# Four-head graph attention: transposed aggregation in 32-column groups, and an order of the engines found by list scheduling

## The chip, the cores and the metric

The kernel runs on one core of one Trainium2 chip. The metric is the device time of one execution in microseconds (us). The program is a straight line of instructions: five engines (TensorE as PE, VectorE as DVE, ScalarE as ACT, GpSimd as POOL, SyncE as SP) each work through a fixed queue and wait for each other by semaphores. On PE a matmul is two instructions, a weight load ("PEld" in the profile) and the matmul itself ("PE"); each fp32 matmul that is no transpose makes two such pairs of records.

## The reference, cut to what matters

Thirty-two batches of 512 nodes with 256 features pass through four graph-attention layers, each with a layer norm ahead of it and a residual sum after it. The change concerns the third layer, which has four heads of 64 features:

```python
    def _L2_gnn_ref(h, adj, W, a):
        N_H, D_F = (4, 64)
        Wh = (h @ W).reshape(h.shape[0], h.shape[1], N_H, D_F)
        ...
        e = s_src[:, :, None, :] + s_dst[:, None, :, :]
        e = jnp.where(e > 0, e, NEG_SLOPE * e)
        e = jnp.where(mask, e, -jnp.inf)
        alpha = jax.nn.softmax(e, axis=2)
        h_out = jnp.einsum('bijh,bjhd->bihd', alpha, Wh)
        ...
        return jax.nn.elu(h_out)
```

For each head, every node i takes an average of the other nodes' 64 features, weighted by a softmax over its neighbours j. The other layers have one head of 256 or 512 features, and the fourth also has two dense layers.

## The kernel before, in words

**Streams.** The batches are dealt out to four streams (`NS = 4`), each with one batch at a time, and started 75 us apart in the program's own time (`LEAD`). `batch`, `layer0` to `layer3` are generators: they emit instructions for a step and yield a time at which the stream wants to go on. The loop at the end of `fast` always advances the stream with the earliest time, so the four batches stand at different layers and their instructions are mixed. The order in which the program is written comes from this; the tile framework then sorts the instructions of each engine by its own simulation, except where `keep_in_program_order` ties one down. [...]

**Attention without a division by the softmax's sum first.** A batch is four tiles of 128 nodes (`NT = 4`). For every head, `weights` makes the matrix of unnormalised weights, `w`, with the source nodes j on the partitions: four DVE instructions of 128x512 (L353), one for each tile j, each the maximum of a row (spread over all partitions) and a column, times the mask. Of the four heads, the first row comes from PE transposes into a PSUM bank, the other three through DRAM (`rows_out`, `spread`) with SP's DMAs. The values `v` carry an exponential factor in column D, so that a matmul with D + 1 columns gives the sum of weights as well.

**Layer 2's aggregation.** For each head and each target tile t, `aggregate` adds up four matmuls over j: `w` (128x128) is the stationary operand, `v` with its 65 columns the moving one. Four tiles t share one PSUM bank. DVE then takes a reciprocal of the four sums (L387) and multiplies (L497) into `ya`, a tile with one buffer of its own. After every second head ACT makes the exponential and the ReLU (L504, L505), and `add_elu` (L405, L406) adds the ELU to `x`.

**Resources shared by all streams.** Eight PSUM banks, two for each stream, where a stream may also use those of an idle stream (`bank`). SBUF buffers of the tag "w" (four, for the weights of all layers), "y" (three), "q" (three), "g", "sums" and others. SP issues all plain DMAs: x, row and spread, sums from the sorted order (L614), the table (L647, L648), and the output (L716). POOL issues the indirect DMAs (L607, L655) and adds the residual of the last layer (L715).

Of the kernel before, what the change touches and what calls it, by code (L numbers as in the profile page):

```python
# [8 lines left out]

# [1 line left out]

# [6 lines left out]
FP = mybir.dt.float32  # L20
BF = mybir.dt.bfloat16
# [3 lines left out]
OP = mybir.AluOpType  # L25
AX = mybir.AxisListType
# [5 lines left out]
TINY = 1.0e-30  # L32
CYCLES = 2400.0

@with_exitstack
def fast(ctx, tc, flag, x, adj, w0, a0, w1, a1, w2, a2, mlp1_w, mlp1_b, mlp2_w, mlp2_b,
         w_fc, a_fc, w_hand, a_hand, out):
# [10 lines left out]
    SLOW = 1.5  # L48
    STRETCH = 2.0

    const = ctx.enter_context(tc.tile_pool(name="const", bufs=1))
    work = ctx.enter_context(tc.tile_pool(name="work", bufs=2))
    psum = ctx.enter_context(tc.tile_pool(name="psum", bufs=1, space=bass.MemoryType.PSUM))
    dram = ctx.enter_context(tc.tile_pool(name="dram", bufs=1, space=bass.MemoryType.DRAM))

    turn = [0]
    begun = [0.0]
# [7 lines left out]
        spent[0] += 4 * max(x.shape[-1], P)  # L65
        nc.tensor.matmul(p, w, x, **flags)  # L66

    def transpose(p, x, i, tied=False):
        spent[0] += 2 * P
        instruction = nc.tensor.transpose(p, x, i)  # L70
        if tied:
            tc.keep_in_program_order(instruction)

    active = set()
    banks = [0]
# [131 lines left out]
    def setup():  # L207

        own = work.tile([P, NT, N], FP, tag="w", name="own", bufs=4)
        nc.vector.tensor_scalar(own, adj_sb, 0.0, None, op0=OP.is_gt)  # L210
        nc.gpsimd.affine_select(
            out=own, in_=own, pattern=[[P, NT], [-1, N]], base=0, channel_multiplier=1,
            compare_op=OP.not_equal, fill=1.0,
        )
        tc.keep_in_program_order(nc.vector.tensor_reduce(differ[:, 0:1], adj_sb, AX.XY, OP.min))
        nc.vector.tensor_scalar(differ[:, 0:1], differ[:, 0:1], 0.0, None, op0=OP.is_lt)
        for j in range(NT):
            turn[0] = NS - 1 - j % (NS - 1)
            p = bank()
            for t in range(NT):  # L220
                transpose(p[:, t * P:(t + 1) * P], own[:, t, j * P:(j + 1) * P], ident, j + t == 0)
            nc.scalar.copy(maskT[:, j, :], p)
        turn[0] = NS - 1
        yield
        yield from finish_w(fetched1, 0.01)


        least = small([1], "rden")
        nc.vector.tensor_reduce(least, diag, AX.X, OP.min)
        nc.vector.tensor_scalar(differ[:, 1:2], least, 0.0, None, op0=OP.is_le)  # L230
        nc.vector.tensor_copy(W2[:, :, :, :D], raw2.rearrange("p k (h d) -> p k h d", d=D))
        nc.vector.tensor_scalar_mul(A2v[:, :, 1:2], A2v[:, :, 0:1], -0.8)
        nc.vector.tensor_scalar_mul(A2v[:, :, 2:3], A2v[:, :, 2:3], 0.8)
        for k in range(KF):
            project(W2[:, k, :, D:], lambda k, f: raw2[:, k, f * P:(f + 1) * P], k, A2)
            yield
        yield from finish_w(fetched3, 0.2)

        for tri, sign in ((before, 1), (after, -1)):
            nc.vector.memset(tri, 1.0)  # L240
            nc.gpsimd.affine_select(
                out=tri, in_=tri, pattern=[[sign, P]], base=0, channel_multiplier=-sign,
                compare_op=OP.is_gt, fill=0.0,
            )
        ties = work.tile([P, 2 * N - P], FP, tag="w", name="ties", bufs=4)
        nc.vector.memset(ties, TINY)
        nc.gpsimd.affine_select(
            out=ties, in_=ties, pattern=[[-1, 2 * N - P]], base=N - P, channel_multiplier=1,
            compare_op=OP.is_gt, fill=0.0,
        )  # L250
        nc.vector.tensor_copy(band, ties)
        yield
        yield from finish_w(fetched4, 0.2)
# [89 lines left out]
    def weights(r_col, t_col, masked=True, r=None):  # L343

        landed = r is not None
        if not landed:
            r = bank()
            for t in range(NT):
                transpose(r[:, t * P:(t + 1) * P], r_col(t).to_broadcast([P, P]), ident)
        wt = work.tile([P, NT, N], FP, tag="w", name="w", bufs=4)  # L350
        for j in range(NT):
            if masked:
                w = nc.vector.scalar_tensor_tensor(  # L353
                    wt[:, j, :], r, t_col(j), maskT[:, j, :], op0=OP.max, op1=OP.mult
                )
                if landed and j == 0:
                    tc.keep_in_program_order(w)
            else:
                nc.vector.tensor_scalar(wt[:, j, :], r, t_col(j), None, op0=OP.max)
        return wt  # L360
# [22 lines left out]
            matmul(p, wt[:, j, t * P:(t + 1) * P], rhs(j), start=(j == 0), stop=(j == NT - 1))  # L383

    def reciprocal(den):
        r = small([1], "rden") if len(den.shape) == 2 else small([NH, 1], "rden4")
        nc.vector.reciprocal(r, den)  # L387
        return r

# [62 lines left out]
    def layer2(xt, xn, rs, when):  # L452
        hT = yield from turned(xn, when)
        v = work.tile([P, NT, NH, CH], FP, tag="v", name="v2", bufs=4)
        for t in range(NT):
            ps = bank()
            for k in range(KF):
                matmul(
                    ps[:, :NH * CH], hT[:, k, t * P:(t + 1) * P], W2[:, k, :, :], start=(k == 0), stop=(k == KF - 1)
                )  # L460
            pv = ps[:, :NH * CH].rearrange("p (h c) -> p h c", c=CH)
            nc.scalar.activation(v[:, t, :, D:], pv[:, :, D:], AF.Exp, scale=rs[:, t:t + 1])
            nc.vector.scalar_tensor_tensor(  # L463
                v[:, t, :, :D], pv[:, :, :D], rs[:, t:t + 1], v[:, t, :, D:D + 1].to_broadcast([P, NH, D]),
                op0=OP.mult, op1=OP.mult,
            )
            yield after_us(0 if t + 1 < NT else 1)
        ya = work.tile([P, NT, F], FP, tag="y4", name="y4", bufs=1)
        wts = []

        def begin(h):
            wts.append(
                weights(
                    lambda t: v[:, t, h, D + 2:D + 3], lambda j: v[:, j, h, D + 1:D + 2], r=far[h]
                )
            )
            return after_us(3.2)

        row_d = rows_out(v[:, :, :, D + 2], NH)
        far = [spread(row_d[h, :]) if h else None for h in range(NH)]
        when = begin(0)
        note(v.rearrange("p t h c -> p (t h) c")[:, :, D:])
        yield after_us(3)
        for h in range(NH):
            last = when
            if h + 1 < NH:
                when = begin(h + 1)
            yield last  # L490
            wt = wts[h]
            p = bank()
            for t in range(NT):
                aggregate(p[:, t * (D + 1):(t + 1) * (D + 1)], wt, t, lambda j: v[:, j, h, :D + 1])
            pv = p[:, :NT * (D + 1)].rearrange("p (t c) -> p t c", c=D + 1)
            r = reciprocal(pv[:, :, D:])
            nc.vector.tensor_tensor(  # L497
                ya[:, :, h * D:(h + 1) * D], pv[:, :, :D], r.to_broadcast([P, NT, D]), op=OP.mult
            )
            if h % 2:  # L500
                c = slice((h - 1) * D, (h + 1) * D)
                y = ya[:, :, c]
                q = pair("q").rearrange("p a (b f) -> p (a b) f", f=2 * D)
                nc.scalar.activation(q, y, AF.Exp)  # L504
                nc.scalar.activation(y, y, AF.Relu)  # L505
                add_elu(xt[:, :, c], y, q)
            yield after_us(0)
        xn, rs = new_xn(), small([NT], "rs")
        for t0 in range(0, NT, 2):
            norm(xt, xn, rs, t0, False)  # L510
        yield after_us(7)
        return xn, rs, after_us(2)
# [50 lines left out]
    def sort_attend(oT, b):  # L563
# [31 lines left out]
            project_half(oT, halves, ends, 1, t)  # L595
            yield after_us(0)
        for t in range(NT):
            junk = work.tile([P, N], BF, tag="junk2", name="junk2", bufs=1)
            nc.scalar.activation(
                junk, tj, AF.Sign, bias=ends[:, t, 2:3], scale=-1.0, accum_out=found[:, 1, t:t + 1]  # L600
            )
# [17 lines left out]
        for c in range(2):  # L619
# [2 lines left out]
            u = sums[:, :, 1, :]  # L622

            T = small([NT], "T")
            tc.keep_in_program_order(nc.vector.tensor_copy(T, u[:, :, F + 1]))
            tot = work.tile([P, C], FP, tag="tot", name="tot", bufs=1)
            nc.vector.tensor_tensor(sums[:, 2, 0, :], u[:, 0, :], u[:, 1, :], op=OP.add)
            nc.vector.tensor_tensor(sums[:, 3, 0, :], sums[:, 2, 0, :], u[:, 2, :], op=OP.add)
            nc.vector.tensor_tensor(tot, sums[:, 3, 0, :], u[:, 3, :], op=OP.add)
# [34 lines left out]
        for t in range(NT):  # L664
# [1 line left out]
            y, q = pair(), pair("q")  # L666
            g = gs[t]
            z = g[:, :2 * C]
            tc.keep_in_program_order(
                nc.vector.scalar_tensor_tensor(z, z, ends[:, t, 2:3], g[:, 2 * C:], op0=OP.mult, op1=OP.add)  # L670
            )
            rd = reciprocal(z[:, F:F + 1])
            z = z.rearrange("p (c n) -> p c n", c=2)[:, :, :F]
            nc.scalar.activation(q, z, AF.Exp, scale=rd)
# [122 lines left out]
    one = const.tile([1, 1], FP, name="one")  # L797
    nc.vector.tensor_reduce(one, p[:1, :P], AX.X, OP.max)
    nc.vector.tensor_scalar(flag, one, 0.5, None, op0=OP.is_gt)


@with_exitstack
# [430 lines left out]
```

## Time and profile before

| What | us |
|---|---|
| median of 3 runs (2934.32 to 2936.52) | 2936.34 |
| span of the profiled execution, first to last instruction | 2929.6 |
| PE busy | 2858.9 |
| PE weight loads busy | 2329.5 |
| DVE busy | 2219.9 |
| ACT busy | 1536.8 |
| POOL busy | 502.3 |

The profile is of one execution; its own time is known as the span, and the profile gives nothing beyond it, so that what lies before the first and after the last instruction can only be taken as the distance to the median, 6.7 us. A line of the profile names the source line, the engine, the operation, the output and input tiles by name, the shape, the count and then busy time and the mean of one in ns, or what the sentence ahead of it says. `L66` is the helper `matmul`, `L70` the helper `transpose`; so PE's rows are told apart by their tiles and shapes. The row of 128x65 (4096 records, mean 273 ns) is layer 2's aggregation. The granted TensorE clock was 0.996 of full speed.

### The profile page before, as it was taken

The page shows a single profiled execution, that of the slowest core. Times are in us where ns is not written, and L with a number is a line of the kernel's source. Part 1 is how long each engine was busy: PE and PEld are TensorE (multiplying, and loading weights), DVE is VectorE, ACT ScalarE, POOL GpSimd, SP SyncE. Part 2 cuts the span into 40 slices and gives each one's busy share as a digit, 9 for nine tenths or more (in the row PEclk, how much of TensorE's full clock was granted, in tenths as well). Part 3 has the DMA queues.
Part 4 walks back from the last instruction along what each step waited for, and adds up shares of the span by engine and source line. Part 5 has one row for each costly group of instructions (what it writes and reads, how often), then busy time and mean ns, then how long its engine had stood idle before and what let it go on. Part 6 is the DMA issues. An engine that isn't in the chain of part 4 may idle for free.

```text
span 2929.6 us, 43083 instructions
## 1 busy us (share of the span) xinstructions
PE 2858.9 (98%) x15177; PEld 2329.5 (80%) x15177; DVE 2219.9 (76%) x5676; ACT 1536.8 (52%) x3922; POOL 502.3 (17%) x515
## 2 busy tenths in 40 slices
PE   8999999999999999999999999999999999999998
PEld 6777887877888877888877888788887788877876
DVE  4677877778778778778778777787787787777764
ACT  4444455555555555555554556545555555555444
POOL 0011112112122111122021121111221111211220
PEclk9999999999999999999999999999999999999999
DMA  3033223233223333233332233222332322323230
GB/s 94 19 102 102 80 88 116 91 98 95 88 94 106 93 100 98 84 102 96 100 102 80 89 115 93 91 97 91 94 116 80 102 93 88 104 93 96 90 107 30
DMA packets 193182, 270.89 MB, mean 92 GB/s; under 512 B 17024, under 2 KB 156094, under 8 KB 192960
## 3 DMA queue, kind: packets, MB, share of 16 engines
q1 hardware_dynamic: 163200, 169.76, 18.5%
q0 software_dynamic: 29760, 98.30, 10.4%
q8 instruction: 123, 2.02, 0.3%
q14 instruction: 99, 0.81, 0.1%
HBM read 152.62 MB, written 115.39 MB: 91 GB/s over the span
## 4 chain that ended last, share of the span: by engine, by line
PE 82%; DVE 10%; ACT 4%; DMA 3%; issue 1%; SPq 0%; POOL 0%; DVEq 0%; POOLq 0%; ACTq 0%
PE b L66 75%; PE b L70 7%; DVE st L269 2%; DMA g<-table,at 2%; DVE sums L641 1%; DVE xn L280 1%; DVE x L406 1%; DVE y L405 1%; ACT v L325 1%; DVE sums L632 1%; ACT y L505 1%; ACT q L504 1%; DVE w L353 1%; ACT hT L290 1%; DVE tot L646 0%
## 5 line engine op out<-in xcount | busy, mean ns | idle before, releaser
L66 PE MATMUL b<-v,w 128*128 128x65 f32 (+1 forms) x7232 | 1218.0, 321 | 10.6 <-DVE w L353 10.5
L66 PEld LDWEIGHTS b<-v,w 128*128 128x128 f32 x7232 | 1050.0, 191 | 168.7 <-issue 56.1
L66 PE MATMUL b<-WFC,oT 128*128 128x256 f32 (+1 forms) x2048 | 495.2, 380 | 0.0
L66 PEld LDWEIGHTS b<-WFC,oT 128*128 128x128 f32 x2048 | 374.5, 189 | 49.3
L66 PE MATMUL b<-W,hT 128*128 128x259 f32 (+1 forms) x1536 | 388.8, 391 | 22.8 <-DVE v L463 14.1
L353 DVE SCALAR_TENSOR_TENSOR w<-b,v,maskT 128x512 f32<-128x512 f32 x512 | 369.4, 744 | 5.1 <-PE b L70 4.1
L607 POOL DMA_INDIRECT order<-v,at x248 | 277.0, 1117 | 490.7 <-DVE oT L730 152.3
L66 PEld LDWEIGHTS b<-W,hT 128*128 128x128 f32 x1536 | 285.3, 192 | 75.3 <-DVE v L463 17.1
L715 POOL TENSOR_TENSOR x<-x,y 128x512 f32<-128x512 f32 x62 | 87.8, 1416 | 1063.7 <-ACT y L713 950.0
L353 DVE SCALAR_TENSOR_TENSOR w<-spread,v,maskT 128x512 f32<-128x512 f32 x384 | 269.5, 742 | 0.0
L66 PE MATMUL b<-hT,WM 128*128 128x512 f32 x512 | 250.0, 599 | 0.7 <-ACT hT L290 0.7
L66 PE MATMUL b<-oT,WM 128*128 128x512 f32 x512 | 231.2, 594 | 0.0
L655 POOL DMA_INDIRECT g<-table,at x124 | 120.9, 975 | 642.8 <-ACT y L675 292.0
L387 DVE RECIPROCAL rden<-b 128x1 f32<-128x1 f32 (+1 forms) x516 | 77.3, 162 | 184.8 <-PE b L66 183.0
L529 ACT ACTIVATE v<-b,ends 128x256 f32<-128x256 f32 x256 | 118.8, 467 | 177.2 <-PE b L66 172.9
L269 DVE BATCH_NORM_STATS2 st<-x 128x6 f32<-128x256 f32 x512 | 193.3, 409 | 6.4 <-DMA x<-in_x_dram 4.1
L412 DVE TENSOR_TENSOR y<-q,y 128x512 f32<-128x512 f32 (+1 forms) x194 | 132.9, 685 | 82.9 <-ACT q L411 45.0
L339 ACT ACTIVATE oT<-b,bias 128x512 f32<-128x512 f32 x128 | 87.7, 686 | 182.7 <-PE b L66 182.0
L290 ACT ACTIVATE hT<-b 128x512 f32<-128x512 f32 x256 | 146.5, 592 | 70.3 <-PE b L70 70.2
L66 PEld LDWEIGHTS b<-oT,WM 128*128 128x128 f32 x512 | 97.5, 191 | 95.7 <-issue 92.4
L70 PE MATMUL b<-ident,xn 128*128 128x128 f32 x1024 | 147.4, 275 | 6.7 <-DVE xn L280 4.0
L70 PEld LDWEIGHTS b<-ident,xn 128*128 128x128 f32 x1024 | 123.7, 143 | 31.9 <-DVE xn L280 5.2
(143 smaller groups left out, 3748.1 us busy)
## 6 DMA issues: line engine op xcount, KB each, us to landing
table<-sums SPq DMA_DIRECT2D x62, 1032.0 KB
sums<-order SPq DMA_DIRECT2D x62, 516.0 KB
spread<-row SPq DMA_DIRECT2D x96, 256.0 KB
x<-in_x_dram SPq DMA_DIRECT2D x32, 512.0 KB
out_dram<-x SPq DMA_DIRECT2D x62, 256.0 KB
sums<-order SPq DMA_DIRECT2D x62, 129.0 KB
order<-v,at POOLq DMA_INDIRECT x248
g<-table,at POOLq DMA_INDIRECT x124
```

The source lines that it names most:

```text
L66: nc.tensor.matmul(p, w, x, **flags)
L70: instruction = nc.tensor.transpose(p, x, i)
L269: nc.vector.bn_stats(st[:, i, :], xt[:, t0 + i, :])
L290: nc.scalar.activation(hT[:, :, t0 * P:(t0 + 2) * P], p.rearrange("p (k n) -> p k n", k=KF), AF.Relu)
L339: nc.scalar.activation(o[:, f, :], p, AF.Relu, bias=bias[:, f:f + 1])
L353: w = nc.vector.scalar_tensor_tensor(wt[:, j, :], r, t_col(j), maskT[:, j, :], op0=OP.max, op1=OP.mult)
L387: nc.vector.reciprocal(r, den)
L412: nc.vector.tensor_tensor(r, q, r, op=OP.add)
L529: nc.scalar.activation(halves[c][:, t, :F], ps[:, :F], AF.Copy, scale=ends[:, t, 0:1])
L607: nc.gpsimd.indirect_dma_start(out=orders[c], out_offset=bass.IndirectOffsetOnAxis(ap=at[:, 0, t:t + 1], axis=0), in_=halves[c][:, t, :], ...
L655: nc.gpsimd.indirect_dma_start(out=g, out_offset=None, in_=table, in_offset=bass.IndirectOffsetOnAxis(ap=at[:, 1, t:t + 1], axis=0),)
L715: (nc.gpsimd if n == 2 else nc.vector).tensor_tensor(xr, xr, y, op=OP.add)
```

## The change

It has two parts. **One:** layer 2's aggregation is turned round. The values become the stationary operand, 32 columns of a head at a time, and the weights `w` (128x512) the moving one. A new helper, `beside`, places such a matmul on one of four groups of 32 columns of the PE array, and its output on 32 partitions of a bank. There are 4 heads x 2 halves of 64 features and 4 sums of weights (column D, repeated 32 times), which makes 12 groups: three runs of four groups, as `plan` lists them. A run is four steps over j with four matmuls each, and needs the weights of two heads. Its result is transposed (features on the partitions), so ACT copies it to SBUF (new tile `y4`, two buffers) and four PE transposes turn it back; DVE's reciprocals and products follow. The products go to tiles of the shared tag "y", and the second head of a pair is multiplied after the next run.

**Two:** at the end of `fast`, `arrange` takes all instructions, works out who needs whose result, gives each a duration from a table of prices, and simulates the five engines: each takes, of the instructions that are ready, the one that stands first in the program. Buffers are handed out in the simulation as they come free; a run's 16 matmuls are kept together. The sequence found is tied down on every engine. The earlier `keep_in_program_order` ties are gone. Along with this, `junk2` shares the buffer of `junk`, and `tot` has two buffers.

In the order of the changed program, PE's 2048 matmuls with 65 columns (4096 records) are replaced by 1536 with 512 columns on 32-column tiles, and the transposes of tiles named y rise from 512 to 896; all other counts on PE are the same.

```diff
+    def beside(p, w, x, c, **flags):
+        spent[0] += 4 * x.shape[-1] * w.shape[-1] // P
+        nc.tensor.matmul(p, w, x, tile_position=(0, c), **flags)
...
-        for h in range(NH):
-            last = when
-            if h + 1 < NH:
-                when = begin(h + 1)
-            yield last
-            wt = wts[h]
+        Q = D // 2
+        plan = (
+            ((0, D), (0, 0), (0, Q), (1, D)),
+            ((1, 0), (1, Q), (2, D), (2, 0)),
+            ((2, Q), (3, 0), (3, Q), (3, D)),
+        )
+        begin()
...
+        when = begin()
+        for g, parts in enumerate(plan):
+            yield when
             p = bank()
+            for j in range(NT):
+                for i, (h, c) in enumerate(parts):
+                    still = v[:, j, h, c:c + Q] if c < D else v[:, j, h, D:D + 1].to_broadcast([P, Q])
+                    beside(
+                        p[i * Q:(i + 1) * Q, :], still, wts[h][:, j, :], i * Q, start=(j == 0), stop=(j == NT - 1)
+                    )
+            s = work.tile([P, N], FP, tag="y4", name="y4", bufs=2)
+            nc.scalar.copy(s, p)
+            yield after_us(0.9)
+            if g < 2:
+                when = begin()
+            p = bank()
             for t in range(NT):
-                aggregate(p[:, t * (D + 1):(t + 1) * (D + 1)], wt, t, lambda j: v[:, j, h, :D + 1])
-            pv = p[:, :NT * (D + 1)].rearrange("p (t c) -> p t c", c=D + 1)
-            r = reciprocal(pv[:, :, D:])
-            nc.vector.tensor_tensor(
-                ya[:, :, h * D:(h + 1) * D], pv[:, :, :D], r.to_broadcast([P, NT, D]), op=OP.mult
-            )
-            if h % 2:
+                transpose(p[:, t * P:(t + 1) * P], s[:, t * P:(t + 1) * P], ident)
+            pv = p.rearrange("p (t c) -> p t c", c=P)
+            r = small([NT, 2], "rden4")
+            sums = [i for i, (h, c) in enumerate(parts) if c == D]
+            for k, i in enumerate(sums):
+                nc.vector.reciprocal(r[:, :, k:k + 1], pv[:, :, i * Q:i * Q + 1])
...
+            if g == 0:
+                y = pair().rearrange("p a (b f) -> p (a b) f", f=2 * D)
+                ends_at = later
+                nc.vector.tensor_tensor(y[:, :, :D], pv[:, :, Q:3 * Q], r[:, :, 0:1].to_broadcast([P, NT, D]), op=OP.mult)
...
-            junk = work.tile([P, N], BF, tag="junk2", name="junk2", bufs=1)
+            junk = work.tile([P, N], BF, tag="junk", name="junk2", bufs=1)
...
-            tc.keep_in_program_order(nc.vector.tensor_copy(T, u[:, :, F + 1]))
-            tot = work.tile([P, C], FP, tag="tot", name="tot", bufs=1)
+            nc.vector.tensor_copy(T, u[:, :, F + 1])
+            tot = work.tile([P, C], FP, tag="tot", name="tot", bufs=2)
...
+    arrange(tc, homes)
```

The core of the new order (`price` gives an instruction its duration; `in_order` simulates; `arrange` ties the result down):

```python
HANDOVER = {"PE": 40.0, "DVE": 33.0, "Activation": 33.0, "Pool": 70.0, "SP": 28.0}
SWITCH = 93.0
...
        job.passes = 2 if whole and not turned else 1
        job.load = 109.0 * elements(still) / P * job.span / P
        job.flow = 109.0 if turned else (elements(moving) * (5.0 / 6.0 if whole else 0.45) + 2.4) * job.span / P
...
    while any(coming.values()) or any(waiting.values()):
        for e in order:
            while coming[e] and coming[e][0][0] <= clock[e]:
                _, rank, place, job = heapq.heappop(coming[e])
                heapq.heappush(waiting[e], (rank, place, job))
        nexts = [(clock[e] if waiting[e] else coming[e][0][0], e) for e in order if waiting[e] or coming[e]]
        at, e = min(nexts)
        job = heapq.heappop(waiting[e])[-1] if waiting[e] else heapq.heappop(coming[e])[-1]
        ...
        put(job, e, at)
...
def arrange(tc, homes):

    jobs, users = jobs_of(list(tc.nc.cur_bb.bb.instructions), homes)
    edge = mybir.DependencyInfo(mybir.DependencyClass.NoSync, mybir.DependencyReason.DATA)
    for line in in_order(jobs, users, homes)[0].values():
        for a, b in zip(line, line[1:]):
            tc.add_manual_dep(b.ins, a.ins.name, edge, reason="arranged")
```

## The prediction

> **What bounds the kernel now.** I read the busy times first, then the busy times by stage, then PE's own waits, and last single rows, for prices.
>
> ```profile
> PE 2858.9 (98%) x15177; PEld 2329.5 (80%) x15177; DVE 2219.9 (76%) x5676; ACT 1536.8 (52%) x3922; POOL 502.3 (17%) x515
> ...
> PE 82%; DVE 10%; ACT 4%; DMA 3%; issue 1%; SPq 0%; POOL 0%; DVEq 0%; POOLq 0%; ACTq 0%
> ```
>
> PE is busy for 98% of the span and carries 82% of the chain that ended last; DVE, next, has 24% in hand. A busy PE need not be a PE at its peak, so the share alone proves little. The stages show how little is idle:
>
> ```profile
> 0.00:300.00 300.00, 277.53 (x1464) 226.00 (x1465) 196.62 (x544) 138.05 (x368) 33.95 (x50) 0.98 0.26 77
> 300.00:2700.00 2400.00, 2368.90 (x12649) 1936.31 (x12648) 1873.44 (x4777) 1284.52 (x3288) 432.62 (x432) 1.00 0.30 96
> 2700.00:2930.00 230.00, 212.42 (x1068) 167.23 (x1066) 149.87 (x356) 114.20 (x268) 35.75 (x34) 0.98 0.24 77
> ```
>
> The first two figures of a row are the stretch and its length, the next PE's busy time. PE is idle for 22.5 us while the streams start, 31.1 us in the 2400 us of the middle, and 17.6 us in the end: 71.2 us in all. A better order can win at most that; fewer PE microseconds are a separate gain, and nearly every one of them counts. PE's waits by cause are small and scattered:
>
> ```profile
> PE b L66 <- DVE v L463: 14.1, 7, 2.9
> PE b L66 <- DVE w L353: 10.5, 18, 0.9
> PE b L70 <- ACT v L325: 9.2, 22, 0.9
> PE b L70 <- DMA W<-in_L_gnn_W_dram: 6.7, 1, 6.7
> ```
>
> So the price of a PE record decides. A record lasts longer than the step to the next, so I take steps from runs of equal records:
>
> ```profile
> 1399.80 3.40 PE L66 MATMUL b<-v,w 128*128 128x65 f32 x29
> ...
> 1415.54 1.88 PE L66 MATMUL b<-hT,WM 128*128 128x512 f32 x4
> ...
> 1411.53 1.03 PE L70 MATMUL b<-ident,xn 128*128 128x128 f32 x8
> ```
>
> A last record of 65 columns lasts 0.273 us (its row's mean), so its step is (3.40 - 0.273)/28 = 0.112 us; another run, 32 records in 3.68 us, gives 0.110, and I use 0.111. With 512 columns (a last record is 0.592 us, the line's median) the step is (1.88 - 0.592)/3 = 0.429 us, and a transpose's (1.03 - 0.275)/7 = 0.108. 512 columns in 0.429 us are 0.84 ns a column, so 65 columns need 0.054 us of flow; at 0.111 us the four-head aggregation waits for weight loads, not for data.
>
> **What the Trainium skill says.** "TensorE: Matmul & The Clock Gate", section LDWEIGHTS: a load takes its columns over 1.2 GHz, 107 ns for 128. The trace agrees: 0.111 us is the step of the 65-column records. The same page, Part 3: matmuls on different tiles of the array run together, the next starting some 4 ns later; three 32-column tiles with 512 rows gained 2.38 times; matmuls start and end strictly in program order. No tile smaller than the array is in this trace. "TensorEngine Tiling (Array Packing)", Key Properties and Restrictions: changing the tiling mode drains the engine, and column tiling excludes transposes of fp32. So each run enters and leaves the mode. Nothing in the trace shows a drain.
>
> **PE, removed.** Per batch 4 heads x 4 tiles x 4 j = 64 matmuls; fp32 makes two records of each, 128 x 0.111 = 14.2 us, 455 us for 32 batches.
>
> **PE, added.** Per batch three runs of 16 matmuls, 32 records of 512 columns each. If four column groups flow together, a run is 8 steps of 0.429 = 3.43 us, three are 10.3. The 12 transposes cost 12 x 0.108 = 1.3. In the changed kernel's PE order all 96 runs stand unbroken, so there are six mode changes per batch at most. A drain is what a record lasts beyond its step, 0.592 - 0.429 = 0.163 us; it lies between nothing (loads go on under it) and 0.163 plus an uncovered load of 0.109. Six cost 1.0 us, 0 to 1.6. Sum 12.6 us.
>
> Net 1.6 us per batch, **52 us** in all; 83 with free changes, 31 with dear ones.
>
> **DVE, ACT.** The rows of the replaced work and of the copy's nearest relative:
>
> ```profile
> L497 DVE TENSOR_TENSOR y<-b,rden 128x256 f32<-128x256 f32 x128 | 53.3, 416 | 1.1
> ...
> L387 DVE RECIPROCAL rden<-b 128x4 f32<-128x4 f32 x128 | 22.7, 177 | 83.5 <-PE b L66 83.4
> ```
>
> ```profile
> L581 ACT COPY tj<-b 128x512 f32<-128x512 f32 x31 | 17.8, 576 | 1.7 <-PE b L70 1.7
> ```
>
> DVE loses 4 x (0.177 + 0.416) = 2.37 us per batch and gets four reciprocals, three products of 256 elements and two of 128 (estimate 0.29 us: L712 takes 680 ns for 512 elements and 422 for 256, so 1 ns an element): 2.53 us, or 5 us more over the program. ACT gets 3 copies of 0.576 us, 55 us more, to some 1592 us (54%). Both lie under PE, and I cost them at nothing: PE has the other three streams' matmuls while a run's copy, transposes and products follow each other (0.6 + 0.6 + 0.6 us). With only one stream, in the first 75 us, that cover is missing: up to 3 x 1.2 us once, which I leave in the range.
>
> **Buffers.** Results now live in the shared "y" buffers (three) from one run to the next, some 5 us, instead of in y4, and a run needs two heads' weights at once, out of four "w" buffers that all layers share. A wait for either would stand in ACT's or DVE's queue with other streams' evictions behind it, and PE behind those. Before, the loop too had the next head's weights begun before a head was aggregated, and DVE waits 5.1 us in all at L353 for anything. I take nothing; the loss is rival two. A second "tot" buffer and one "junk" for ACT and DVE instead of two: each once per batch or so, gain and loss under DVE's and ACT's spare time, nothing.
>
> **The order.** List scheduling reorders all five queues; none of it is work, so it can only change the 71.2 us of idle PE, plus bubbles inside "busy". About 7 us of the start are the first weights' arrival and stay. In the middle the causes are v, w and hT coming late from DVE and ACT, just what an order can move. On POOL the same indirect DMAs stand in nearly the same sequence; on SP the out_dram stores (L716) now stand between table and sums transfers. SP already waits 480.6 us at L716 for POOL's addition, and PE doesn't feel it, as each stream's gathers have the other streams' matmuls beside them. If that cover were gone, the gathers behind would be late by the store's wait, up to 51.6 us (its longest). Bounds: 45 us won, 50 lost; I take **20 won**: 16, half of the middle, and 4 of the ends.
>
> **Sum.** 2929.6 - 52 - 20 = 2857.6 us of span. The page gives no total of the profiled execution beyond its span; the median 2936.34 (of 2934.32 to 2936.52) is 6.7 us above it, and I keep that as what lies around the span: 2864 us, 2.5% less.
>
> **Rivals.**
> *One: the two records of an fp32 matmul serialize the groups (slower).* Each matmul is a pair of records, and a pair's second must follow its first on the same columns. If PE also starts records strictly in order, the next group's first record starts beside this one's second, and only two flow at once. A run is then 17 steps of 0.429 = 7.3 us, three are 21.9, with transposes and changes 24.2 against 14.2: +10.0 x 32 = 320 us. With 20 won: 2936 + 320 - 20 = 3236 us. For it: the trace always shows both records in succession, and the strict order above. Against it: the second page's Key Properties, by which tiles run independently. It decides from a run of (14.2 - 2.3)/3 = 3.97 us, 0.25 us per matmul.
> *Two: runs wait.* PE is in order, so a run whose second head is not ready stops all streams. A row of weights takes DVE 0.744 us (L353), a run's j-step 0.86, so a run started on its first row needn't stall; yet one row late in each of 96 runs is 71 us. With nothing won by the order: 2936 - 52 + 71 = 2955 us. It decides from 0.54 us per run. Against it: DVE is 24% idle.
> *Three: the order does more.* 45 us won and free changes: 2936 - 83 - 45 = 2808 us.
>
> **Numbers.** Likeliest 2864 (four groups together; its own range 2808 to 2912): 0.77, rival three being its lower edge. Rival one 0.13, rival two 0.10. A change within 0.2% (5.9 us), about what a measurement of this kernel can tell from none, comes only from half-way cases of rival two. Faster 0.77, within 0.2% 0.05, slower 0.18. The range, 2808 to 2945, leaves out rival one (0.13), the worst of rival two (0.04) and 0.03 below it.
>
> **What would show it.** Right: 1536 x 2 records of 512 columns on 32-column tiles, in groups of four starting within some 10 ns, 16 matmuls in about 3.4 us; the row of 65 columns gone; 896 transposes of y where there were 512; PE busy some 50 us less; ACT some 55 us more; PE's idle in the middle 10 to 20 us. Wrong: runs of 7 us (rival one); PE waiting for w or v at the run's line for tens of us (rival two); gaps of over 0.3 us around each run; a middle idle beyond 31 us, which fells the order's gain.

## The result, and the profile after

| What | before | after |
|---|---|---|
| median in one comparison, us | 2935.33 (2933.96 to 2936.52) | 2890.03 (2889.89 to 2893.93, four runs) |
| span of the profiled execution, us | 2929.6 | 2888.2 |
| PE busy, us | 2858.9 | 2807.9 |
| PE idle in the span, us | 70.7 | 80.3 |

The ratio of the times is 0.9848, 95% interval 0.9834 to 0.9862: 45 us less (1.5%). The forecast was 72 us less. The time lies in the forecast range, in the direction forecast, but 26 us above the number. The two lines of the page that answer to those of before:

```profile
PE 2807.9 (97%) x14537; PEld 1990.1 (69%) x14537; DVE 2203.1 (76%) x5708; ACT 1602.2 (55%) x4018; POOL 506.7 (18%) x515
...
PE 78%; DVE 17%; ACT 2%; DMA 2%; issue 1%; SPq 0%; POOL 0%; DVEq 0%; POOLq 0%
```

PE is busy for 51 us less, as forecast ("some 50"), but it now carries 78% of the chain that ended last, not 82%, and DVE 17%, not 10%. The busy times by stage (stretch, length, then busy time and count of PE, PEld, DVE, ACT, POOL, the granted clock, the DMA share and GB/s), cut so that the ends are as long as before:

```profile
0.00:300.00 300.00, 265.56 (x1395) 192.22 (x1396) 200.99 (x551) 141.47 (x369) 34.22 (x47) 0.98 0.25 77
300.00:2660.00 2360.00, 2329.57 (x12095) 1646.67 (x12095) 1851.34 (x4796) 1338.75 (x3370) 432.79 (x429) 1.00 0.30 97
2660.00:2889.00 229.00, 212.79 (x1050) 151.25 (x1048) 150.75 (x362) 121.99 (x281) 39.69 (x39) 0.97 0.26 85
```

PE idles 34.4 us at the start (22.5 before), 30.4 in the middle (31.1) and 16.2 in the end (17.6). So the list scheduling, which was to cut the idle time by 20 us, shows no cut at all in this kernel, and the start has become 12 us worse. PE's waits by cause (in total, times, longest):

```profile
PE b L352 <- ACT hT L578: 13.2, 19, 0.8
PE b L360 <- POOL own L499: 8.9, 1, 8.9
PE b L360 <- DVE xn L568: 7.9, 10, 2.3
...
PE b L352 <- ACT y L726: 5.6, 7, 0.8
PE b L352 <- DVE w L641: 5.1, 5, 2.0
```

In this kernel L352 is `matmul`, L356 `beside` and L360 `transpose`. Two things are new. One wait of 8.9 us, for POOL's mask, comes once, at the start. The others are short and regular: ACT's y at L726 is waited for seven times, once per round of four batches (some 350 us), and in the middle (300 to 2660 us) hT 13 times. They are not at `beside`: its own row shows 0.9 us of idle time before it in the whole program. So the runs do not wait for their weights, which rejects rival two, but something else in each round now comes late. It shows in other layers: L726 is the second layer's ReLU, hT at L578 any layer's transposed input.

The turned aggregation in the timeline (start, length, then the group; x32 are the 16 matmuls of a run):

```profile
1531.34 1.03 PE L352 MATMUL b<-v,w 128*128 128x257 f32 x4
1532.30 3.64 PE L356 MATMUL b<-w,v 128*32 128x512 f32 x32
1535.87 1.13 PE L352 MATMUL b<-v,w 128*128 128x257 f32 x4
```

From the start of the run to the start of what follows it are 3.57 us: about 3.43 of steps and 0.14 for a longer first step and for leaving the mode. Rival one, which needed 7.3 us, is rejected too. The groups of instructions that the sum had priced (count, then busy time, mean ns, and idle time before):

```profile
L356 PE MATMUL b<-w,v 128*32 128x512 f32 x3072 | 350.8, 595 | 0.9 <-DVE w L641 0.9
...
L785 ACT COPY y<-b 128x512 f32<-128x512 f32 x96 | 56.0, 583 | 140.1 <-PE b L356 138.7
...
L801 DVE TENSOR_TENSOR y<-b,rden 128x256 f32<-128x256 f32 x32 | 13.4, 418 | 0.0
...
L806 DVE TENSOR_TENSOR y<-b,rden 128x128 f32<-128x128 f32 x32 | 9.0, 281 | 0.0
```

The copy takes 583 ns (576 assumed), the products 418 and 281 (416 and 290). Each of these prices is met within some 3%. The time that is missing is not in them.

### The profile page after: what moved, and what is told of

Read it like the earlier page. It is cut to its first block, busy times and chain, and to the rows that moved or that the text cites. A ratio compares the mean times of both kernels' runs of the same rounds, so it can differ in the third digit from the quotient of the medians.

```text
span 2888.2 us, 41950 instructions
## 1 busy us (share of the span) xinstructions
PE 2807.9 (97%) x14537; PEld 1990.1 (69%) x14537; DVE 2203.1 (76%) x5708; ACT 1602.2 (55%) x4018; POOL 506.7 (18%) x515
## 4 chain that ended last, share of the span: by engine, by line
PE 78%; DVE 17%; ACT 2%; DMA 2%; issue 1%; SPq 0%; POOL 0%; DVEq 0%; POOLq 0%
PE b L352 59%; PE b L356 10%; PE b L360 9%; DVE w L641 7%; DVE st L557 1%; DVE xn L568 1%; DVE oT L1037 1%; DVE junk L895 1%; DVE y L691 1%; DVE x L692 1%; DMA row<-row 1%; DVE y L698 1%; DMA spread<-row 1%; DVE sums L953 1%; ACT hT L578 1%
## 5 line engine op out<-in xcount | busy, mean ns | idle before, releaser
L352 PE MATMUL b<-v,w 128*128 128x257 f32 (+1 forms) x3136 | 758.2, 384 | 15.8 <-ACT y L726 5.6
L352 PEld LDWEIGHTS b<-v,w 128*128 128x128 f32 x3136 | 576.1, 190 | 164.2 <-issue 47.2
L352 PE MATMUL b<-WFC,oT 128*128 128x256 f32 (+1 forms) x2048 | 487.1, 380 | 0.0
L352 PEld LDWEIGHTS b<-WFC,oT 128*128 128x128 f32 x2048 | 375.4, 189 | 56.6 <-issue 3.0
L352 PE MATMUL b<-W,hT 128*128 128x259 f32 (+1 forms) x1536 | 380.6, 386 | 4.5 <-ACT v L613 2.5
L641 DVE SCALAR_TENSOR_TENSOR w<-b,v,maskT 128x512 f32<-128x512 f32 x512 | 352.8, 743 | 20.6 <-PE b L360 19.8
L356 PE MATMUL b<-w,v 128*32 128x512 f32 x3072 | 350.8, 595 | 0.9 <-DVE w L641 0.9
L352 PEld LDWEIGHTS b<-W,hT 128*128 128x128 f32 x1536 | 280.6, 190 | 65.1 <-issue 17.2
L352 PE MATMUL b<-hT,WM 128*128 128x512 f32 x512 | 245.1, 599 | 11.2 <-ACT hT L578 11.2
L1022 POOL TENSOR_TENSOR x<-x,y 128x512 f32<-128x512 f32 x62 | 78.9, 1272 | 916.0 <-ACT y L1020 858.2
L352 PE MATMUL b<-oT,WM 128*128 128x512 f32 x512 | 231.8, 596 | 2.5 <-DVE oT L1037 2.5
L356 PEld LDWEIGHTS b<-w,v 128*32 128x32 f32 x3072 | 90.5, 109 | 207.6 <-issue 201.5
L578 ACT ACTIVATE hT<-b 128x512 f32<-128x512 f32 x256 | 149.5, 601 | 50.6 <-PE b L360 49.8
L360 PE MATMUL b<-ident,xn 128*128 128x128 f32 x1024 | 157.7, 279 | 13.7 <-DVE xn L568 7.9
L352 PEld LDWEIGHTS b<-oT,WM 128*128 128x128 f32 x512 | 95.6, 190 | 107.3 <-issue 99.9
L360 PEld LDWEIGHTS b<-ident,xn 128*128 128x128 f32 x1024 | 122.7, 142 | 63.9 <-issue 23.1
```

What stands on the lines that cost most here:

```text
L356: nc.tensor.matmul(p, w, x, tile_position=(0, c), **flags)
L578: nc.scalar.activation(hT[:, :, t0 * P:(t0 + 2) * P], p.rearrange("p (k n) -> p k n", k=KF), AF.Relu)
L641: nc.vector.scalar_tensor_tensor(wt[:, j, :], r, t_col(j), maskT[:, j, :], op0=OP.max, op1=OP.mult)
L1022: (nc.gpsimd if n == 2 else nc.vector).tensor_tensor(xr, xr, y, op=OP.add)
```

## The experiments

Each ratio is to the kernel before, run in turn with it on one chip, with a 95% interval; `e3_group_by_group` alone was run once and has none. The kernel before came out at 2934 to 2936 us each time, so medians of different experiments are compared with each other too.

### The two parts apart

`e2_order_only` keeps `arrange`, the shared `junk` and the second `tot`, and puts back the old loop over heads with 65 columns. `e1_turned_only` has the new loop over runs, and the framework's order, ties, `junk` and `tot` of before.

```diff
# e2_order_only, against the kernel after
-        for g, parts in enumerate(plan):
...
+        for h in range(NH):
...
+                aggregate(p[:, t * (D + 1):(t + 1) * (D + 1)], wt, t, lambda j: v[:, j, h, :D + 1])
# e1_turned_only, against the kernel after
-    arrange(tc, homes)
...
```

> The list scheduling alone: the old aggregation of 65 columns, all queues ordered by the simulation. Theory: PE's idle stays as large in the middle and grows by 12 us in the start, as in the changed kernel (34.4 us against 22.5 in the first 300 us): 2935 + 10 = 2945 us. Rival (the prediction's step, an order wins 20 us of idle PE): 2915 us.

> The transposed aggregation alone: no list scheduling, the framework sorts as before and the old ties are back. In this order the 96 runs of tile matmuls stand in 150 pieces, 50 of them whole, many of one to three matmuls. Theory: the list order is worth little as an order, its worth is that it keeps the runs whole. A piece costs one entry and exit (0.285 us in the trace of the changed kernel: 92 + 23 + 170 ns) and rounds its matmuls up to groups of four: 437 groups instead of 384, 53 x 0.858 = 45 us, and 54 x 0.285 = 15 us; the start is 12 us better than in the changed kernel. Expected 2890 + 60 - 12 = 2938 us, no faster than before. Rival (pieces cost nothing; order and aggregation simply add up, and the order lost 10 us): 2936 - 52 = 2884 us.

Measured:

| aggregation | order of the framework | list scheduling |
|---|---|---|
| 65 columns | 2935 us | 2876.29 us, 0.9801 [0.9784, 0.9818] |
| turned | 3016.28 us, 1.0279 [1.0263, 1.0296] | 2890.03 us, 0.9848 [0.9834, 0.9862] |

The theory held missed both (2945 us for the order, 2938 for the aggregation). **The order alone wins 59 us; the aggregation, which was to take work from PE, costs 81 us in the old order and 14 in the new one.** All of the 45 us are the order's. The line of the busy times for the same 2340 us (300 to 2640) of four kernels, first before:

```profile
300.00:2640.00 2340.00, 2309.30 (x12369) 1890.46 (x12368) 1829.04 (x4659) 1252.49 (x3202) 425.64 (x425) 1.00 0.30 96
```

`e2_order_only`:

```profile
300.00:2640.00 2340.00, 2339.76 (x12594) 1930.16 (x12593) 1880.26 (x4757) 1277.40 (x3264) 430.20 (x427) 1.00 0.30 98
```

`e1_turned_only`:

```profile
300.00:2640.00 2340.00, 2274.10 (x11494) 1563.62 (x11483) 1762.83 (x4542) 1272.90 (x3195) 404.66 (x412) 1.00 0.29 93
```

The kernel after:

```profile
300.00:2640.00 2340.00, 2310.12 (x12012) 1633.11 (x12012) 1833.85 (x4748) 1325.29 (x3333) 430.25 (x427) 1.00 0.30 97
```

PE idles for 30.7 us before, 0.2 with the order alone, 65.9 with the aggregation alone and 29.9 with both. With the order alone the idle time of the middle is gone altogether, and PE does 225 more records in the same stretch. Its page shows how much of the gain was hidden from the idle time:

```profile
PE 2835.3 (98%) x15177; PEld 2333.8 (81%) x15177; DVE 2239.5 (78%) x5676; ACT 1538.7 (53%) x3922; POOL 505.0 (18%) x515
```

The same 15177 records are busy 23.6 us less than before: short gaps between records that count as busy, since a record is shown longer than the step to the next. (By starts of records in the trace, PE spends some 65 us of the middle's 2400 beyond its records' usual steps before, and some 16 of 2350 with the order alone.) With the span's 2879.3 us, idle time fell by 26.7 us to 44.0; the two make the 50 us by which this profiled span is shorter.

From the order alone to both, the same account runs the other way: some 51 us of PE work go (below), but PE's busy time falls by only 27.4 (2835.3 to 2807.9), and its idle time rises by 36.3 (44.0 to 80.3). So 60 us come back, 24 as short gaps and 36 as idle time.

### Do the four groups need their order?

`e3_group_by_group` issues the matmuls of one group after another.

```diff
-            for j in range(NT):
-                for i, (h, c) in enumerate(parts):
+            for i, (h, c) in enumerate(parts):
+                for j in range(NT):
```

> The changed kernel with the 16 matmuls of a run written group by group (four j of one column group, then the next group) instead of j by j. Theory: column groups flow together only where PE meets them one after the other in its queue; now eight records of one group follow each other, so a run takes some 29 to 32 steps of 0.429 = 12.4 to 13.7 us instead of 3.6, 96 x 9 to 10 = 860 to 970 us more: about 3800 us. Rival (PE fetches work for a free column group from further down its queue): a run stays near 3.6 us and the time near 2890 us. In between (it looks a few records ahead, as rival one of the prediction had it for neighbours): a run of 7 to 10 us, 3220 to 3500 us.

Measured: 3378.04 us, in one execution: the case in between. A run in its timeline:

```profile
1503.79 8.86 PE L356 MATMUL b<-w,v 128*32 128x512 f32 x32
1512.58 0.66 PE L360 MATMUL b<-ident,y 128*128 128x128 f32 x4
```

Start to start a run is 8.79 us, about 20 steps of 0.429, where the kernel after has 8 steps in 3.57. 96 x 5.22 = 501 us more work; 488 were measured. Full serial order would be 32 steps. The trace does not name a record's group, but the starts fall into four chains of eight records, 429 ns or a little more apart, and the first record of each is the longer one (617 ns against 592), as in the kernel after. In the median over the 96 runs the first chain starts at 0, 453, 882, 1312, 1741, 2170, 2599 and 3028 ns, and the second at 1747: ahead of three of the first group's records, which stand earlier in the program. So PE doesn't wait for a record whose columns are taken; it goes past it, by three records here, and not much further, or all four groups would have started together. With j outside, as in the change, the next group is always within reach.

### The start

At the start of the kernel after, PE (first fence) and POOL (second) in the timeline, with what a wait was for in brackets:

```profile
7.92 1.84 PE L352 MATMUL b<-W0a,wT 128*128 128x3 f32 x8
18.63 2.91 PE L360 MATMUL b<-ident,own 128*128 128x128 f32 x12 [8.87 <-POOL own L499]
```

```profile
16.32 0.22 POOL L399 TENSOR_SCALAR W1a<-W1a 128x2 f32<-128x2 f32 x1 [12.59 <-DMA W1a<-in_L_gnn_a_dram]
...
16.65 1.92 POOL L499 TENSOR_SCALAR_AFFINE_SELECT own<-own 128x2048 f32<-128x2048 f32 x1
```

POOL makes the mask `own` at L499 at 16.65 us. It is behind two scalings of W1a, whose DMA ends at 16.3 us; the price table has 2.25 us for that DMA, so the order had put the scaling first. PE in turn stands at the mask's transposes, which the order had put ahead of the first batch's, since x is priced at 10 us, and the first x lands after 4.1 (issued at 1.82, landed at 5.90; the expectation below has 4.7, which no trace shows). `e5_start_prices` is the kernel after with prices for the first 200 instructions as the trace has them; `e8_order_start` is `e2_order_only` with the same edit.

```diff
+        if job.place < 200 and e == "SP":
+            job.took = {"x": 4700.0, "adj": 8000.0, "W1a": 8500.0, "raw": 5700.0, "diag": 3100.0}.get(kind, job.took)
...
+        if job.place < 200 and e == "SP" and kind != "W0a" and (kind.endswith("a") or kind == "A"):
+            job.holds = 1700.0 if kind != "A" else 800.0
...
-        t = 1271.0 if op == "TensorTensor" and n > 48 else 250.0
+        t = 1271.0 if op == "TensorTensor" and n > 48 else 180.0 + 0.85 * n if op == "TensorScalarAffineSelect" else 250.0
```

> The changed kernel with other prices for the loads of the start alone, as its trace shows them: the first x 4.7 us to landing instead of 10, adj 8 instead of 5, W1a 8.5 instead of 2.25, the column loads' issue 1.7 us instead of 0.4, and POOL's select of the mask 1.9 us instead of 0.25. The order that comes out has the first batch's norm ahead of the mask and POOL's select ahead of the additions that wait for W1a. Theory: the start's loss against before (PE idle 34.4 us against 22.5 in the first 300 us) is these prices: 10 to 12 us off, 2879 us. Rival (the first stream's lead is given back later, since the four streams share PE anyway): 2888 to 2892 us.

> The list scheduling alone (old aggregation of 65 columns, 2876 us) with the start's prices: the same correction that brought the turned kernel from 2890 to 2884. Theory: the start's order is independent of the layer, so 6 us less: 2870 us. Rival: its middle is dense already, and a lead of the first stream changes how the streams lie: 2870 to 2890 us.

Measured: 2884.24 us, 0.9828 [0.9812, 0.9844], and 2870.01 us, 0.9775 [0.9752, 0.9797]. Both are 6 us below the kernel that they start from, though the intervals overlap with those. The stage of `e5_start_prices` says where:

```profile
0.00:300.00 300.00, 273.32 (x1424) 197.16 (x1428) 203.23 (x558) 145.07 (x379) 35.96 (x50) 0.97 0.26 80
```

PE idles 26.7 us there instead of 34.4, 7.7 less, and the wait for the mask is gone. The cause is confirmed, at about half the size expected: 4 us of the start's 12 remain, and of the 7.7 some 6 reach the end. The list order alone has that wait too (8.8 us), so it belongs to the new order and not to the aggregation.

### Whole runs or pieces

The framework's order breaks the runs: in PE's order of `e1_turned_only` other matmuls stand between a run's own, so that the 96 runs lie in 150 pieces, and 437 groups of at most four matmuls, where 384 would do. `e12_loose_runs` tests pieces within list scheduling. It is `e7_lead73`, below (start prices, LEAD 73), with the rule off that keeps a run together: 147 pieces, 427 groups.

```diff
-        if job.span < P and block is not None and block.span == job.span and block.fills == job.fills:
+        if False:
```

> The kernel with start's prices and LEAD 73, with the list scheduling no longer keeping a run's 16 matmuls together. In its order the 96 runs stand in 147 pieces, 62 of them whole, which hold 427 groups of four or fewer instead of 384. Theory pieces: 43 x 0.858 + 51 x 0.285 = 37 + 15 = 52 us, 2920 us (2900 if part of it falls into PE's idle). Rival (the 81 us that the turned aggregation lost in the framework's order were its waits, and pieces are cheap): 2868 to 2880 us.

Measured: 2923.39 us, 0.9966 [0.9959, 0.9973], which is 55 us above `e7_lead73`. The row of the run's matmuls, whole runs first:

```profile
L360 PE MATMUL b<-w,v 128*32 128x512 f32 x3072 | 350.4, 595 | 0.2 <-DVE oT L1041 0.2
```

```profile
L360 PE MATMUL b<-w,v 128*32 128x512 f32 x3072 | 396.0, 596 | 4.4 <-DVE w L645 4.3
```

The same records are busy 46 us longer. A group that is not full takes its two steps all the same: up to the start of what follows, a piece of one matmul takes 0.976 us, one of four 0.997. So (427 - 384) x 0.858 = 37 us, and 51 further entries and exits at 0.31 (the mean in the kernel after, worked out under "PE work" below) are 16: 53 us. The price of pieces is confirmed. In `e1_turned_only` it makes 53 x 0.858 + 54 x 0.31 = 62 us, and the row there shows 409.5 us, 59 above the whole runs'. So the aggregation alone took no work from PE on balance: it saved 51 us and lost 62. That is 62 of the 132 us by which it misses its gain (81 and 51); PE's idle time is up by another 49 (119.7 us of the span against 70.7), and the rest, some 20, is again short gaps.

### The streams' spacing

LEAD, the distance at which the streams are started in the program's own time, was 75 us with the old aggregation, and stayed. A batch's PE work is shorter now, so the streams may meet at other places. LEAD 73 and 70 were tried on `e5_start_prices`; LEAD 70 on `e8_order_start` and `e1_turned_only`.

```diff
-LEAD = 75.0
+LEAD = 70.0
```

> The changed kernel with the start's prices (2884 us) and one number more: the streams start 70 us apart in the program's time (LEAD) instead of 75. The list scheduling alone left PE idle for 0.2 us in 2350 us of the middle, with the turned aggregation it is 30.8 of 2360, at waits that return in every round of four batches. Theory spacing: how the four streams' layers lie over each other decides whether PE always finds ready work; 75 us fits the old aggregation, and the turned one, which is shorter, needs another distance. Expected 2855 to 2870 us, PE's idle in the middle below 20 us. Rival structure: the runs' copies, transposes and products, or the shared buffers, hold the streams up at any distance: 2880 to 2890 us.

> As before with LEAD 73. Theory spacing: the time changes by tens of us with the distance, not smoothly; here 2855 to 2870 us as at 70. Rival structure: 2880 to 2890 us.

> The same (list scheduling, old aggregation, start's prices) with LEAD 70. Theory spacing: 75 us suits the old aggregation, 70 does not; PE goes idle in the middle and the time rises by 30 to 50 us: 2900 to 2920 us. Rival structure (spacing hardly matters, the queues reorder themselves): within 6 us of the kernel with 75.

> The turned aggregation in the framework's own order (3016 us at LEAD 75), with LEAD 70. Its runs then stand in 120 pieces with 408 groups, against 150 and 437: pieces cost 28 us instead of 60. Theory pieces: 32 us less, 2984 us. Rival (spacing is the larger part there too): a change by 50 us or more in either direction, as between 70 and 75 with the old aggregation under list scheduling (2870 to 2941 us).

| kernel | LEAD 75 | 73 | 70 |
|---|---|---|---|
| turned, list order, start prices | 2884.24 | 2867.95, 0.9761 [0.9739, 0.9783] | 2872.08, 0.9777 [0.9755, 0.9799] |
| 65 columns, list order, start prices | 2870.01 | not run | 2940.89, 1.0015 [1.0007, 1.0023] |
| turned, framework's order | 3016.28 | not run | 3138.23, 1.0708 [1.0681, 1.0735] |

Five microseconds of LEAD are worth 12 us less for one aggregation and 71 us more for the other: the order's gain is lost again. So a change of LEAD has effects of the size sought. It also changes the order in which the whole program is written, and with it every queue, and no run separates the two. Of the expectations, LEAD 70 came out just above its range (2872 for 2855 to 2870), with 22.9 us of idle time where less than 20 was expected, LEAD 73 in its range, and `e9_order_lead70` lost more than expected. What the two with losses wait for, PE's waits of `e9_order_lead70` and then of `e13_turned_lead70` (waited for, in total, times, longest):

```profile
PE b L356 <- DVE w L645: 21.4, 30, 1.8
```

```profile
PE b L66 <- DVE w L357: 76.8, 28, 8.6
```

In both it is weights from DVE, but the trace gives two different reasons. In `e9_order_lead70` it is 21.4 us on this line, where `e8_order_start` has 2.1. Half of them is one wait of some 1.6 us in every round, and DVE is busy all through it: while PE waits up to 589.3 us, DVE works on ELU and norm steps and one row of w. That streams meet in their attention steps at this spacing is the likely reading; no run isolated it. These waits are also only a part: between `e8_order_start` and `e9_order_lead70` the span grows by 70 us (2868.6 to 2938.3), of which 39 are again short gaps inside PE's busy time (2833.8 to 2872.3).

In `e13_turned_lead70` it is 76.8 us, where `e1_turned_only` has 12.9 on that line, and eight of the waits, those over 5 us, one in every round, make 57 of them. Just ahead of each of the eight DVE had itself stood idle as long, for a DMA of the fourth layer's sorted sums. One of the eight, DVE first:

```profile
1023.79 0.43 DVE L654 TENSOR_TENSOR sums<-sums 128x258 f32<-128x258 f32 x1 [8.58 <-DMA sums<-order]
```

```profile
1024.93 2.51 PE L66 MATMUL b<-v,w 128*128 128x257 f32 x5 [8.58 <-DVE w L357]
```

The weights come next in DVE's queue, behind the sums, and PE behind the weights. Why the DMA is late in that order was not tested. Pieces are not what this kernel loses by: they fall to 120, and to 408 groups, 34 us less work by the prices above, and the time rises by 122 us (its granted clock was 0.97, against 0.994 in `e1_turned_only`, so that a part of this may be clock).

### Buffers, and a last version

Two more on `e7_lead73` and `e5_start_prices`: a fourth "y" buffer, with one "y4" less (`e10_y4buffers`), and LEAD 70 with the streams' steps stretched a little more (`e11_lead70_stretch`).

```diff
# e10_y4buffers, against e7_lead73
-        wT = work.tile([P, N], FP, tag="y", name="wT", bufs=3)
+        wT = work.tile([P, N], FP, tag="y", name="wT", bufs=4)
...
-        return work.tile([P, 2, F], FP, tag=tag, name=tag, bufs=3)
+        return work.tile([P, 2, F], FP, tag=tag, name=tag, bufs=4 if tag == "y" else 3)
...
-            s = work.tile([P, N], FP, tag="y4", name="y4", bufs=2)
+            s = work.tile([P, N], FP, tag="y4", name="y4", bufs=1)

# e11_lead70_stretch, against e5_start_prices
-LEAD = 75.0
+LEAD = 70.0
...
-STRETCH = 2.0
+STRETCH = 2.2
```

> The kernel with start's prices and LEAD 73 (2868 us) with a fourth buffer for the shared tag y, paid for by one buffer less for y4. It tests whether the turned layer, which now keeps results in y from one run to the next, makes other streams wait. Theory spacing: the y buffers hold nobody up, 2866 to 2870 us. Rival (buffers): PE's idle in the middle (25 us of 2340) comes from ACT and DVE waiting for a y tile, and 5 to 15 us go: 2853 to 2863 us.

> The kernel with start's prices, LEAD 70 and STRETCH 2.2 (the factor by which the streams' clock counts PE time; 2.0 elsewhere). Another way in which the four streams lie over each other, a candidate for a version faster than all before. Theory spacing: somewhere between 2855 and 2870 us, with PE's idle in the middle at or under 25 us. Rival structure: no choice gets under the 2868 us of LEAD 73.

Measured: 2865.72 us, 0.9772 [0.9754, 0.979], for the buffers: no difference that can be told from `e7_lead73`. So a "y" buffer more, paid for with a "y4", wins nothing; whether each alone would count was not run. And 2859.69 us, 0.9754 [0.9736, 0.9773], for the stretch: the fastest median of all, with an interval that overlaps with those of LEAD 73 and of `e8_order_start`. In its middle PE still idles for 25.1 us:

```profile
300.00:2640.00 2340.00, 2314.95 (x12030) 1652.11 (x12029) 1863.01 (x4776) 1325.37 (x3368) 421.38 (x426) 1.00 0.30 97
```

All the turned kernels in list order do (22.9 to 30.8 us), at each spacing tried, where the old aggregation idles for 0.2 and 0.3 us at LEAD 75. Between the best medians found for each, 2860 and 2870, the turned aggregation is worth some 10 us of the 51 us that it takes from PE, and the overlap of the intervals leaves even that unsure. Whether that is the longer chain of copy, transposes and products, or only a spacing not found yet, stays open: the old aggregation was run at two spacings, the turned one at four settings.

## Why the prediction was right or wrong, point by point

**PE work: right.** In the trace's records, from start to start, 454.5 us of 65-column steps went (455 forecast). A run has 8 steps: its four groups start at 0, 7, 13 and 20 ns, the next four at 453, then every 429. From the start of a run to the start of what follows are 345 us for the 96 runs; 384 transposes at 0.109 add 42, and some 17 lie ahead of the runs and in the record after them. Net about 51 us; 52 were forecast. Entering takes 0.093 us and the first step 23 ns more, leaving 0.114 us and then 0.056 on the next record where that is a transpose (46 of the runs), 0.104 where it is not. That is 0.29 or 0.33 us a run, where the expectations above used 0.285 for all, and 30 us in all, where two times 0.163 made 31.

**DVE, ACT: right as prices, wrong as "nothing".** ACT is busy 65 us more (55 forecast), DVE 17 us less (5 more; the difference lies in rows that the change does not touch, such as xn, 97.2 us at L276 and 79.2 at L564 now), and neither is near full. But the cover that the prediction named, the other streams' matmuls, is there only when another stream is ready. That it isn't always is seen in the short regular waits, and in what LEAD does. Which link of the chain of copy, transposes and products is late was not isolated. DVE's queue has one new wait in the middle, 17.6 us for the rows of weights that come by DMA (`spread`), in six waits, where the order alone has none; the turned layer needs the second head's row before its first run. But only one wait of PE, the 0.9 us at `beside`, follows from it at once, and in `e11_lead70_stretch`, where it is 5.4 us, PE idles 25.1 us all the same. So it is not shown to carry the loss.

**Buffers: right, as far as tested.** `e10_y4buffers` wins nothing by a "y" buffer more, and PE waits 0.9 us for weights at `beside`. The number of "w" buffers was not changed in any run.

**The order: two errors.** The bound of 45 us came from the idle time, with the bubbles inside "busy" named and then given no number; they alone were 24 us, and with the old aggregation the order wins 59 us. And the start: 4 us were to be won in the ends, but the start lost 12, some 8 of it through the prices of DMAs on the new order's list. The prediction had read the start's 7 us of first weights, and not asked what the list schedule knows of DMAs there.

**The sum: the step that failed.** -52 and -20 were added as if each held beside the other. By the two-by-two table the parts are -59 (order) and +81 (aggregation) alone, and -45 together; beside the new order the aggregation is +14, not -52. Of the +81, some 62 are broken runs, which the new order keeps whole; that the aggregation leans on the order in this way the sum did not say. Less work on a busy engine counts only if other work is ready in its place; in these streams, 75 us apart, that depends on where they meet, as the runs with other LEADs show for the size and not for the mechanism. The sentence "nearly every one of them counts" had been read off an idle time of 1.3% in the middle. It was true for the work, not for the schedule. That the sum came within 26 us is luck in part: the order was taken 39 us too low, and the aggregation 66 us too high.

**PE busy was no evidence.** "PE busy some 50 us less" came out at 51, and seemed to confirm the sum. The order alone gives -24 and the work -51: 75, of which 24 came back as short gaps.

**The rivals.** One and two are rejected by the timeline and by the waits. The slower side was real, as `e1_turned_only` shows, but through broken runs and the order of the streams, which no rival named. Strict order of records, on which rival one rested, isn't what `e3_group_by_group` shows.

## What to carry to other kernels

When a change has two parts, build each alone before adding their gains: here the part that was to remove 51 us of work cost time beside either order, and the part that removed none gave the whole gain. After a change of one stage in staggered streams, set the stagger anew, and measure it, since 5 us of it moved the time by up to 71 under list scheduling. Keep matmuls on column groups together in whole runs with neighbours on different groups, and give a list scheduler measured DMA times for the start, where nothing covers a wrong one.

## What the runs showed of the hardware

- Four fp32 matmuls on 32-column groups flow together at the full rate, though each is two records: a lone matmul took 0.976 us up to the next start, four on different groups 0.997 (`e12_loose_runs`). The Trainium skill, "TensorE: Matmul & The Clock Gate", Part 3, has 2.38 times for three groups; this trace has about four for four, within a run: 32 records in 8 steps of 0.429 us.
- The same Part says that matmuls start in program order. `e3_group_by_group` shows a record starting before three earlier ones, whose columns were busy (1747 ns against 2170 to 3028). Here the measurement decides.
- "TensorEngine Tiling (Array Packing)", Key Properties, says that a change of the tiling mode drains the engine, without a price. The trace agrees that each change costs time, 0.29 to 0.33 us to enter and leave with the records used here; that it is a drain the trace does not show.
- At the start of the kernel after, the loads on SP's queue landed in the order of their issue. W0a, the first, took 2.1 us from issue to landing. W1a, no larger, took 8.5 us (7.8 to 16.3): it landed behind adj, three x and W, which had landed at 10.9 to 16.1. The first x took 4.1 us, the other three 9.0 to 10.8.
- PE's busy share hides short gaps: the same 15177 records are busy for 23.6 us less in another order (2858.9 and 2835.3 us).
